# Four attention tiles: transposing on VectorE from 32x32 squares loaded from DRAM

## The chip, the cores and the metric

The kernel runs on one core of one Trainium2 chip. The metric is the device time of one execution in microseconds, as the median of several runs. The profiled execution is a further run, recorded by the hardware profiler; its span goes from the first to the last instruction of the core.

## The reference

Two layers act on 2,048 rows of 1,024 float32 numbers (4 batches of 512):

```
attn = einsum('ds,td->st', w1, w2) * sparse_mask
y    = gelu(einsum('bds,st->bdt', x, attn) + b2)          # exact gelu
x    = layernorm(x + y)
w_l  = dequant_kbit(qweight, lut4, 4)                     # 4 bit planes, 16 values per output row
y    = where(norm(x) > 64, x @ w_h.T, x @ w_l.T) + bias   # w_h: the same with 8 bits
out  = layernorm(x + y)
```

Each row of x is treated on its own, so the order in which a tile holds its rows does not matter as long as the rows come out where they belong.

## The kernel before

**Tiles.** The rows are 16 tiles of 128 (n = 0 to 15), each an SBUF tile `x{n}` with a row per partition, which is loaded once and kept until it is stored. Every tile goes through "attention" (the first layer) and through the second layer. The 1,024 columns are KT = 8 blocks of 128.

**Before the tiles.** In the first 55 us or so the masked product of w1 and w2 is made, only in a band around the diagonal (`attn`), because the mask is zero elsewhere; that it is zero outside the band is checked separately (`check_outside`, L448: a strip of the mask is loaded into a tile called `raw` and its absolute values are summed on ScalarE, L455). The second layer's weights are unpacked from bit planes on ScalarE, VectorE and GpSimd and transposed into `wT`.

**Attention of a tile** (`attention`, L489). Its x must stand transposed, with the contracted columns on the partitions. `transposed` (L438) makes `xT` by eight TensorE transposes into PSUM (L263) and two copies of 128x512 by ScalarE (L264). Then come 20 products with the band (L467, "band" below), the bias added by VectorE (L493, tile `z`), gelu on ScalarE (L494), the residual sum with its row total on VectorE (L498), and the layer norm's numbers: minus the mean (L351, VectorE), the sum of squares (L354, ScalarE, tile `junk`), one over the root (L356 and L357, GpSimd). The row is normalized by L361 on VectorE, which the code keeps in a list (`later`) and issues at a later place (`now()`).

**Second layer.** Tiles 0 to 3 go by halves of the output columns: `ffn_half` has eight products of 128x512 (L512), then VectorE adds the bias and x (L524). The left halves run among the early attention tiles, the right halves R0 to R3 alternate with the attention of tiles 12 to 15; after each right half VectorE makes a sum of weight blocks (L573, 128x2048) which the later tiles need. Tiles 4 to 15 go two at a time (`ffn_pair`, L619) with seven products of half size instead of eight (28 matmuls of L629 a pair, into PSUM tiles u, v and w). Their transposed inputs are made by `squares` (L575): VectorE transposes 32x32 squares within each group of 32 partitions (L579), the result goes to DRAM and comes back with the squares at the partitions where they belong (L583, L589), and ScalarE, VectorE and GpSimd copy, add and subtract them (L611 to L616).

**What sets the order.** A scheduler places the instructions of each engine from the order of the code and its own estimates; from the attention of tile 8 on, VectorE alone keeps the order of the code. Each engine runs its own instructions in order. The loop at L711 goes through `todo`; in each turn it first prepares the transposed input of the next entry. So at the turn of a right half the input of the following attention tile is made.

All loads of x and of the mask strips, the trips of the squares and the stores go through SP's queue in the order in which they stand there; each of these transfers has 128 or 32 rows as its outermost size. Tiles 12 to 15 of x are loaded at the turn of tile 10 (L721), into space that the unpacking has left. In SP's order the mask strips of 186 and 570 columns stand ahead of these loads and those of 314 and 442 columns behind them. The products of attention and of the right halves share two PSUM buffers (`mm`) in turn: a band needs the buffer of the band before, which L493 frees, and a right half the one before, which L524 frees.

Of the kernel before, what the change touches and what calls it, by code (L numbers as in the profile page):

```python
# [9 lines left out]
FP = mybir.dt.float32  # L10
# [7 lines left out]
P = 128  # L18
D = 1024
SOON = 12  # L20
PAIR = 2
KT = D // P
# [8 lines left out]
SQ = 32  # L31
Q = P // SQ
# [160 lines left out]
def kernel(  # L193
# [13 lines left out]
    nc = tc.nc  # L207
    x = x.flatten_outer_dims()
    out = out.flatten_outer_dims()
    NT = x.shape[0] // P  # L210
# [4 lines left out]
    with ExitStack() as main:  # L215
# [42 lines left out]
        def transpose_blocks(dst, block):  # L258

            for g in range(NH):  # L260
                pt = ps_tr.tile([P, HALF // P, P], FP, tag="tr", name="pt")
                for j in range(HALF // P):
                    nc.tensor.transpose(pt[:, j, :], block(g * (HALF // P) + j), ident)  # L263
                nc.scalar.copy(dst[:, g * (HALF // P) : (g + 1) * (HALF // P), :], pt)  # L264

        def transpose_columns(dst, src):
            transpose_blocks(dst, lambda k: src[:, ts(k, P)])
# [60 lines left out]
        def transpose_pending(left):  # L328

            while len(pending) > left:  # L330
                ot, w_nat = pending.pop(0)
                transpose_columns(wT[:, :, ts(ot, P)], w_nat)
# [9 lines left out]
        def steps(n):  # L342
            for _ in range(n):
                next(low, None)


        def stats(u, total):


            nm = work.tile([P, 1], FP, tag="nm", name="nm", bufs=4)  # L350
            nc.vector.tensor_scalar(nm, total, -1.0 / D, None, ALU.mult)  # L351
            junk = work.tile([P, D], BF, tag="junk", name="junk", bufs=1)
            ss = work.tile([P, 1], FP, tag="ss", name="ss", bufs=4)
            nc.scalar.activation(junk, u, AF.Square, bias=nm, accum_out=ss)  # L354
            r = work.tile([P, 1], FP, tag="r", name="r", bufs=4)
            nc.gpsimd.tensor_scalar(r, ss, 1.0 / D, EPS, ALU.mult, ALU.add)  # L356
            nc.gpsimd.tensor_tensor(r, r, minus_half, ALU.pow)  # L357
            return nm, r, ss

        def normalize(dst, u, nm, r):  # L360
            nc.vector.tensor_scalar(dst, u, nm, r, ALU.add, ALU.mult)  # L361

        x_tiles = []

        def load_x(pool, n):
            t = pool.tile([P, D], FP, tag=f"x{n}", name=f"x{n}")
            nc.sync.dma_start(out=t, in_=x[ts(n, P), :])
            x_tiles.append(t)

        attn = band.tile([P, KT, WIN], FP, name="attn")  # L370


        with tc.tile_pool(name="prod", bufs=1) as prod:
# [36 lines left out]
            for n in range(AHEAD):  # L410
                load_x(xp0, n)
# [3 lines left out]
            for s in range(KT):  # L415
# [4 lines left out]
                for k in range(KT):  # L420
                    nc.tensor.matmul(  # L421
                        out=ps[:, : hi - lo],
# [11 lines left out]
        for n in range(AHEAD, SOON):  # L434
            load_x(late, n)
        nc.sync.dma_start(out=bias_bc, in_=bias.partition_broadcast(P))

        def transposed(n, tag, bufs, by_bit):  # L438
            xT = late.tile([P, KT, P], FP, tag=tag, name="xT", bufs=bufs)
            if by_bit:  # L440
                cols = x_tiles[n].rearrange("t (b s) -> t s b", s=8)
                transpose_blocks(xT, lambda k: cols[:, k, :])
            else:
                transpose_columns(xT, x_tiles[n])
            return xT


        def check_outside(s):  # L448

            lo, hi = window(s)  # L450
            raw = work.tile([P, D], FP, tag="z", name="raw", bufs=2)
            for i, (a, b) in enumerate(((0, lo), (hi, D))):
                if a < b:
                    nc.sync.dma_start(out=raw[:, a:b], in_=sparse_mask[ts(s, P), a:b])
                    nc.scalar.activation(  # L455
                        raw[:, a:b], raw[:, a:b], AF.Abs, accum_out=outside[:, 2 * s + i : 2 * s + i + 1]
                    )
# [24 lines left out]
        def now():  # L482
            while later:
                later.pop(0)()
# [4 lines left out]
        def attention(n, xT, meanwhile=nothing):  # L489
            xt = x_tiles[n]  # L490
            ps = band_rows(xT)
            z = work.tile([P, D], FP, tag="z", name="z", bufs=2)
            nc.vector.tensor_tensor(z, ps, b2_bc, ALU.add)  # L493
            nc.scalar.activation(z, z, AF.Gelu)  # L494
            now()
            meanwhile()
            total = work.tile([P, 1], FP, tag="total", name="total", bufs=4)
            nc.vector.scalar_tensor_tensor(xt, z, 1.0, xt, ALU.mult, ALU.add, accum_out=total)  # L498
            nm, r, ss = stats(xt, total)

            def rest():
                normalize(xt, xt, nm, r)

                nc.gpsimd.tensor_tensor(ssq[:, n : n + 1], r, r, ALU.mult)
                nc.gpsimd.tensor_tensor(ssq[:, n : n + 1], ssq[:, n : n + 1], ss, ALU.mult)

            later.append(rest)
# [26 lines left out]
        def finish_rows(n):  # L534
            y = x_tiles[n]
            total = work.tile([P, 1], FP, tag="total", name="total", bufs=4)
            nc.vector.tensor_tensor(total, sums[:, n, 0:1], sums[:, n, 1:2], ALU.add)
            nm, r, _ = stats(y, total)

            def rest():  # L540
                if n < EARLY:
                    o = last.tile([P, D], FP, tag="o", name="o")
                else:
                    o = work.tile([P, D], FP, tag="z", name="o", bufs=2)
                normalize(o, y, nm, r)
                nc.sync.dma_start(out=out[ts(n, P), :], in_=o)

            later.append(rest)

        def ffn_half(n, xT, h):  # L550
            ps = ps_mm.tile([P, D], FP, tag="mm", name="mm")
            product(ps[:, :HALF], xT, h)
            now()
            combine(n, h, ps[:, :HALF], bias_bc[:, ts(h, HALF)])
            if h == 1:
                finish_rows(n)
# [11 lines left out]
        def weight_sum(pool, i):  # L568

            plus, minus = sums_of[i]  # L570
            weights[i] = pool.tile([P, KH, HALF], FP, tag=f"t{i}", name=f"t{i}")
            minus = weights[minus] if isinstance(minus, int) else minus
            nc.vector.tensor_tensor(weights[i], plus, minus, ALU.subtract)  # L573
# [112 lines left out]
        unpack_after = [("attention", 1), ("left", 0), ("attention", 4), ("left", 1)]  # L686
        unpack_after += [("attention", 5), ("left", 2), ("attention", 6), ("left", 3)]

        kept = {}
        rows, blocks = {}, {}  # L690

        def prepare_pair(n, part):

            if n == NT:
                return
            if part < PAIR:
                rows[n + part] = squares(last, n + part)
            else:
                blocks[n] = pair_inputs(last, n, rows[n], rows[n + 1])

        def prepare(what, n):
            if what == "attention":
                return transposed(n, "xT", 2, False)
            if what == "left":
                kept[n] = transposed(n, f"early{n}", 1, True)
            return kept[n]
# [4 lines left out]
        for i, (what, n) in enumerate(todo):  # L711
            if (what, n) == ("left", 0):
                transpose_pending(0)
            if (what, n) == ("attention", 2 * EARLY):
                ordered.enter_context(tc.manual_schedule(engines={mybir.EngineType.DVE}))
            if (what, n) == ("attention", SOON - 2):
                steps(100)
                transpose_pending(0)
                first_sb.close()
                last = main.enter_context(tc.tile_pool(name="last", bufs=1, side="right"))  # L720
                for m in range(SOON, NT):  # L721
                    load_x(last, m)
            xT = ready
            if i + 1 < len(todo):
                ready = prepare(*todo[i + 1])
            if what == "attention":
                if n >= SOON + 1:
                    attention(n, xT, lambda: prepare_pair(EARLY, n - SOON - 1))
                else:
                    attention(n, xT)  # L730
                if n < 2 * EARLY:
                    now()
                if n > 8 and checks < KT:
                    check_outside(checks)
                    checks += 1
            else:
                ffn_half(n, xT, 0 if what == "left" else 1)
                if what == "left" and n > 1:
                    check_outside(checks)
                    checks += 1  # L740
                if what == "right":
                    weight_sum(last, n + 1)
                    now()
            if (what, n) in unpack_after:
                steps(1)
# [57 lines left out]
```

## Time and profile before

| | |
|---|---|
| median of 3 runs | 366.83 us (366.29 to 367.3) |
| the profiled execution | 366.59 us, its span 364.7 us |
| mean granted TensorE clock | 0.966 |
| busy share: TensorE, its weight loads, VectorE, ScalarE, GpSimd | 90%, 55%, 63%, 46%, 23% |
| 8 transposes of an attention tile (L263) and their 2 copies (L264) | 1.04 and 1.04 to 1.07 us in the timeline |
| VectorE transpose L579, 128x1024 float32 | 12 times, 2.03 us in the median |
| loads of x, 512 KB each | 16 times, 6.5 us from issue to landing in the median |
| stores, 512 KB each | 16 times, 2.6 us |

A row of the timeline or of the busy times gives the start and the length in us, the engine, the line of the kernel, the operation with its output and inputs, and in brackets how long the engine had been idle and what ended that. A row by stage gives the stretch, its length, the busy times of PE, PEld (weight loads), DVE, ACT and POOL with the number of instructions, the granted clock, the DMA engines' busy share and GB/s. A row of the chain of waits gives start, length, engine, what it wrote and the line; the chain is followed back from the last instruction, at each step to what released it, or to the instruction before it on its engine. A row of the queues gives packets, MB and the packets' time as a share of 16 DMA engines over the span. PE is TensorE, DVE VectorE, ACT ScalarE, POOL GpSimd.

### The profile page before, as it was taken

Reading aid. Unit: us, or ns where it says so; the run is one execution under the profiler, and the core shown is the slowest. Engines: PE = TensorE matmul, PEld = TensorE weight load, DVE = VectorE, ACT = ScalarE, POOL = GpSimd, SP = SyncE. Lnnn points to the kernel's source line nnn. Section 1 sums busy time; section 2 is a strip of 40 time slices with the busy share of each in tenths; the row PEclk is TensorE's granted clock in tenths of the full one; section 3 lists DMA queues with packets and bytes.
Section 4 is the critical chain, followed back from the end, with each engine's and each line's share of the span. In section 5 each row is a group of like instructions: output and inputs, shape, how many; then the busy total and the mean of one; then the engine's idle time right before and its main releaser. Section 6 shows DMA issues by size and latency. Waiting matters only on the chain.

```text
span 364.7 us, 3670 instructions
## 1 busy us (share of the span) xinstructions
PE 328.5 (90%) x1202; PEld 202.1 (55%) x1202; DVE 231.1 (63%) x351; ACT 166.3 (46%) x242; POOL 83.5 (23%) x130
## 2 busy tenths in 40 slices
PE   4599977989999997999999888999999999999970
PEld 3488866876566586866665433443444444444430
DVE  2589887887988997367676854564635526634130
ACT  0994983989649975675444411301212112012011
POOL 0600420454054111212312440401203004013000
PEclk9699998999999999699999999999999999999995
DMA  9997407700011000812154315143251451432003
GB/s 224 333 373 238 162 2 290 286 2 0 3 46 43 0 3 6 309 44 100 39 176 158 120 58 173 58 177 112 115 180 50 175 170 58 173 117 115 1 4 121
DMA packets 28347, 43.90 MB, mean 120 GB/s; under 512 B 7584, under 2 KB 20640, under 8 KB 28320
## 3 DMA queue, kind: packets, MB, share of 16 engines
q1 hardware_dynamic: 23056, 43.00, 33.3%
q10 hardware_dynamic: 5264, 0.59, 1.2%
q8 instruction: 11, 0.18, 0.2%
q14 instruction: 16, 0.13, 0.1%
HBM read 28.90 MB, written 14.68 MB: 119 GB/s over the span
## 4 chain that ended last, share of the span: by engine, by line
PE 34%; DVE 27%; ACT 16%; issue 8%; DMA 6%; POOL 5%; SPq 1%; ACTq 1%; POOLq 0%; DVEq 0%
PE u L629 16%; PE w L629 8%; ACT junk L354 7%; DVE x L498 5%; PE v L629 4%; DMA rows<-there 3%; DVE e L310 3%; PE mm L467 3%; ACT e L303 3%; DVE z L493 3%; POOL r L357 2%; POOL r L356 2%; DVE root L312 2%; DVE root L311 2%; ACT z L494 2%
## 5 line engine op out<-in xcount | busy, mean ns | idle before, releaser
L354 ACT ACTIVATE junk<-x,nm 128x1024 bf16<-128x1024 f32 x32 | 36.8, 1148 | 66.2 <-DVE nm L351 63.9
L467 PE MATMUL mm<-attn,xT 128*128 128x198 f32 (+2 forms) x320 | 63.7, 357 | 3.0 <-ACT xT L264 3.0
L467 PEld LDWEIGHTS mm<-attn,xT 128*128 128x128 f32 x320 | 55.6, 200 | 10.4 <-ACT xT L264 3.2
L303 ACT ACTIVATE e<-v,lt,diff 128x1024 f32<-128x1024 uint8 x48 | 56.7, 1238 | 6.1 <-DVE v L278 6.1
L512 PE MATMUL mm<-wT,xT 128*128 128x512 f32 x128 | 56.5, 594 | 0.6 <-DVE x L524 0.6
L629 PE MATMUL u<-t,halves 128*128 128x512 f32 x96 | 43.3, 594 | 1.0 <-DVE x L649 1.0
L356 POOL TENSOR_SCALAR r<-ss 128x1 f32<-128x1 f32 x32 | 11.5, 359 | 123.9 <-ACT junk L354 123.9
L512 PEld LDWEIGHTS mm<-wT,xT 128*128 128x128 f32 x128 | 23.7, 190 | 27.7 <-issue 27.4
L307 POOL TENSOR_SCALAR root<-v,diff,lt 128x1024 f32<-128x1024 uint8 x16 | 24.3, 1524 | 58.6 <-DVE v L278 44.0
L629 PEld LDWEIGHTS u<-t,halves 128*128 128x128 f32 x96 | 18.1, 190 | 24.6 <-issue 22.8
L611 ACT COPY halves<-rows 128x1024 f32<-128x1024 f32 x6 | 6.3, 1042 | 55.6 <-DMA rows<-there 55.6
L579 DVE STREAM_TRANSPOSE squares<-x 128x1024 f32<-128x1024 f32 x12 | 24.3, 2026 | 11.5 <-DMA there<-squares 11.5
L421 PE MATMUL mm<-w2T,w_sb 128*128 128x268 f32 (+1 forms) x128 | 30.0, 391 | 0.0
L615 POOL TENSOR_TENSOR halves<-halves 128x512 f32<-128x512 f32 x6 | 9.5, 1584 | 85.4 <-DVE halves L612 85.4
L263 PE MATMUL pt<-ident,x 128*128 128x128 f32 x160 | 22.4, 284 | 7.0 <-ACT wT L264 6.4
L421 PEld LDWEIGHTS mm<-w2T,w_sb 128*128 128x128 f32 x128 | 24.9, 203 | 3.1
L361 DVE TENSOR_SCALAR x<-x,nm,r 128x1024 f32<-128x1024 f32 x16 | 13.0, 812 | 20.4 <-POOL r L357 15.8
L311 DVE COPY_PREDICATED root<-v,e 128x1024 f32<-128x1024 uint8 x16 | 22.5, 1405 | 5.3 <-ACT e L303 4.0
L264 ACT COPY xT<-pt 128x512 f32<-128x512 f32 x40 | 21.0, 585 | 10.3 <-PE pt L263 7.2
L498 DVE SCALAR_TENSOR_TENSOR x<-z,x 128x1024 f32<-128x1024 f32 x16 | 21.5, 1342 | 5.3 <-ACT z L494 5.3
L263 PEld LDWEIGHTS pt<-ident,x 128*128 128x128 f32 x160 | 19.2, 155 | 10.0 <-ACT wT L264 7.8
L494 ACT ACTIVATE z<-z 128x1024 f32<-128x1024 f32 x16 | 16.9, 1054 | 15.8 <-DVE z L493 15.8
(71 smaller groups left out, 434.3 us busy)
## 6 DMA issues: line engine op xcount, KB each, us to landing
x<-in_L_attn_x_dram SPq DMA_DIRECT2D x16, 512.0 KB, 6.5
out_dram<-o SPq DMA_DIRECT2D x16, 512.0 KB, 2.6
there<-squares SPq DMA_DIRECT2D x12, 512.0 KB, 3.0
rows<-there SPq DMA_DIRECT2D x48, 128.0 KB, 2.9
w_raw<-in_L_attn_w_dram SPq DMA_DIRECT2D x8, 512.0 KB, 5.2
w_sb<-in_L_attn_w_dram SPq DMA_DIRECT2D x3, 1024.0 KB, 7.4
w_sb<-in_L_attn_w_dram SPq DMA_DIRECT2D x2, 512.0 KB, 4.9
raw<-_L_attn_sparse_mask_dram SPq DMA_DIRECT2D x2, 413.0 KB, 3.3
```

What stands on the lines that cost most here:

```text
L263: nc.tensor.transpose(pt[:, j, :], block(g * (HALF // P) + j), ident)
L303: nc.scalar.activation(entry[j], plane(0), AF.Identity, scale=d_k, bias=l_k)
L307: nc.gpsimd.tensor_scalar(entry[j], plane(0), d_k, l_k, ALU.mult, ALU.add)
L311: nc.vector.copy_predicated(root, plane(1), entry[1])
L354: nc.scalar.activation(junk, u, AF.Square, bias=nm, accum_out=ss)
L421: nc.tensor.matmul(out=ps[:, : hi - lo], lhsT=w1_sb[s][:, k, :], rhs=w2T[:, k, lo:hi], start=(k == 0), stop=(k == KT - 1),)
L467: nc.tensor.matmul(out=ps[:, a:b], lhsT=xT[:, s, :], rhs=attn[:, s, a - lo : b - lo], start=h not in fresh, stop=hi == D or (h == 0 and wi ...
L494: nc.scalar.activation(z, z, AF.Gelu)
L498: nc.vector.scalar_tensor_tensor(xt, z, 1.0, xt, ALU.mult, ALU.add, accum_out=total)
L512: nc.tensor.matmul(out=ps, lhsT=xT[:, k, :], rhs=wT[:, k, ts(h, HALF)], start=(k == 0), stop=(k == KT - 1),)
L579: nc.vector.transpose(out=t, in_=x_tiles[n].rearrange("t (c j k) -> t c k j", c=Q, k=KT))
L629: nc.tensor.matmul(out=ps, lhsT=a[:, k, :], rhs=b[:, k, :], start=start and k == 0, stop=stop and k == KH - 1, skip_group_check=True,)
```

## The change

For tiles 12 to 15 (SOON = 12), `transposed` no longer uses TensorE and ScalarE. x is loaded a second time, by four loads per tile, each to 32 partitions: partition group g gets, of every four 32-column blocks, the g-th (32 rows x 32 columns pieces of 128 bytes), for the rows 4 i + a with a = 0 to 3 one after the other in the free dimension. VectorE then transposes all 32x32 squares in one instruction, which yields columns on partitions with the tile's rows in the order (a, i). The ordinary tiles `x12` to `x15` are loaded in the same row order, by a rearranged view of DRAM, and their results stored through the same view. Two tiles of squares share one buffer with the weight sums t3 and t4, which are written later. No computation is left out.

```
+        def rows_of(dram, n):
+            rows = dram[ts(n, P), :]
+            return rows if n < SOON else rows.rearrange("(i a) d -> a i d", a=Q)
+
         def load_x(pool, n):
             t = pool.tile([P, D], FP, tag=f"x{n}", name=f"x{n}")
-            nc.sync.dma_start(out=t, in_=x[ts(n, P), :])
+            nc.sync.dma_start(out=t, in_=rows_of(x, n))
             x_tiles.append(t)
+
+        def load_squares(t, n):
+            cols = x[ts(n, P), :].rearrange("(i a) d -> i (a d)", a=Q)
+            cols = cols.rearrange("i (m g j) -> g i m j", g=Q, j=SQ)
+            for g in range(Q):
+                nc.sync.dma_start(
+                    out=t[ts(g, SQ), :].rearrange("i (m j) -> i m j", j=SQ), in_=cols[g]
+                )
...
             xT = late.tile([P, KT, P], FP, tag=tag, name="xT", bufs=bufs)
+            if n >= SOON:
+                nc.vector.transpose(
+                    out=xT.rearrange("p k (a i) -> p a k i", a=Q),
+                    in_=in_squares[n].rearrange("p (a k j) -> p a k j", a=Q, k=KT),
+                )
+                return xT
...
-                nc.sync.dma_start(out=out[ts(n, P), :], in_=o)
+                nc.sync.dma_start(out=rows_of(out, n), in_=o)
...
-                for m in range(SOON, NT):
-                    load_x(last, m)
+                for m in range(SOON, NT, 2):
+                    t = last.tile([P, 2, D], FP, tag=f"t{3 + (m - SOON) // 2}", name="in_squares")
+                    for j in range(2):
+                        in_squares[m + j] = t[:, j, :]
+                        load_squares(in_squares[m + j], m + j)
+                        load_x(last, m + j)
```

More of the change, by code (lines that the diff above doesn't have):

```diff
@@ L687 @@
         unpack_after += [("attention", 5), ("left", 2), ("attention", 6), ("left", 3)]
-        kept = {}
+        kept, in_squares = {}, {}
         rows, blocks = {}, {}
```

## The prediction

> **What bounds the kernel now.** I read the page's slices first (TensorE busy everywhere, its clock granted in full from slice 18 on), then the busy time by stage around the change. The row for one round of a right half and an attention tile:
>
> ```profile
> 165.00:176.40 11.40, 11.40 (x45) 7.20 (x44) 7.16 (x12) 5.61 (x11) 2.72 (x7) 1.00 0.23 80
> ```
>
> TensorE (first figure after the length) is busy for all 11.40 us, so its transposes look like time. The chain of waits says otherwise:
>
> ```profile
> 161.12 1.24 DVE x L498 x2
> 162.98 0.72 issue
> 164.84 0.81 DVE x L361
> 165.65 0.62 DVE x L524 x2
> 166.75 1.25 ACT junk L354 x2
> 168.08 0.81 POOL r L356
> ...
> 170.28 1.23 DVE z L493
> 171.53 1.07 ACT z L494
> 172.62 1.24 DVE x L498 x2
> ```
>
> From 157 to 202 us the chain runs through VectorE, ScalarE and GpSimd and never through TensorE. It goes round once per tile: the L524 that closes a half starts at 165.56, 177.07, 189.29 and 201.50, rounds of 11.51, 12.22 and 12.21 us, while TensorE's bands start 11.33 to 11.34 us apart (165.09, 176.43, 187.76, 199.10). The ring is the slower one already. VectorE's and ScalarE's timelines for tile 11:
>
> ```profile
> 162.38 0.15 DVE L351 TENSOR_SCALAR nm<-total 128x1 f32<-128x1 f32 x1
> 164.84 0.81 DVE L361 TENSOR_SCALAR x<-x,nm,r 128x1024 f32<-128x1024 f32 x1 [2.30 <-POOL r L357]
> ```
> ```profile
> 159.95 0.18 ACT L455 ACTIVATION_READ_ACCUMULATOR raw<-raw 128x1 f32 x1
> 160.04 1.04 ACT L494 ACTIVATE z<-z 128x1024 f32<-128x1024 f32 x1
> 160.99 1.04 ACT L264 COPY xT<-pt 128x512 f32<-128x512 f32 x2
> 162.65 1.15 ACT L354 ACTIVATE junk<-x,nm 128x1024 bf16<-128x1024 f32 x1 [0.62 <-DVE nm L351]
> ```
>
> Between L351 and L361 VectorE idles 2.30 us for the squares' sum (L354) and the root on GpSimd. And ScalarE, in order, sums a mask strip (L455, "raw") just ahead of this work.
>
> **What goes.** Four times eight transposes: a band's start to the next product's was 3.59 + 0.87 us, so 0.87 each, 3.5 us of TensorE, and eight copies of 0.585 us on ScalarE. TensorE's round falls to 10.47 us; the ring's does not. I count only the head start before the first round: without tile 12's transposes the half ends 0.9 us sooner, and the gelu of tile 11 no longer waits behind the strip: the ring could begin 0.9 us earlier.
>
> **The new VectorE transpose.** Nearest row: L579, the same 32x32 transpose of 128x1024 float32, 2.03 us. In the changed program's order it stands after L351 and ahead of L361, in the idle 2.30 us, so it costs nothing; without that cover it would be 4 x 2.03 = 8.1 us. If its runs of 32 make it half as slow again (3.0), 4 x 0.7 = +2.8; if it is as quick as L498 (1.23), nothing, since L361 still waits for GpSimd.
> But GpSimd's L356, due 1.60 us after L351, now runs beside it. This row warns:
>
> ```profile
> 168.08 0.80 POOL L356 TENSOR_SCALAR r<-ss 128x1 f32<-128x1 f32 x1 [2.39 <-ACT junk L354]
> ```
>
> L356 takes 0.19 us alone (175.49), and 0.80 beside L573, ending with it. If the transpose held it too, L361 would come 0.5 us later, four times: +2.0. The Trainium skill (SBUF — State Buffer, Who interferes with whom) says that a VectorE instruction blocks GpSimd when it reads two tensors in SBUF or runs in a two-port mode, not with one input outside such a mode. L573 reads two; the transpose reads one, and at 2.03 us against L361's 0.81 for the same elements it is in no fast mode. I take 0 and keep 2.0 for the range.
>
> **The loads.** Four x loads become 16 loads of squares and four x loads, all on SP, from 145.38. Issued at some 0.45 us (four took 1.79), they keep SP for 9 us instead of 1.8, and behind them stand the loads of the strip that tile 11 waits for (314 and 442 columns), on SP and on the same rings. Queue shares:
>
> ```profile
> q1 hardware_dynamic: 23056, 43.00, 33.3%
> q10 hardware_dynamic: 5264, 0.59, 1.2%
> ```
>
> q10 carries almost only the codes' 128-byte packets: 0.012 x 16 x 364.7 us / 5264 = 13 ns each. A load of squares has 1,024 such packets, 64 per engine: 0.85 us; 16 of them 13.6. From 8.3 to 9.3 us that queue moved 1,654 packets, 9.7 ns each on 16 engines: 9.9 us in all. I take the middle, 11.7. An x load, by the transfers between 146.5 and 154.5 us (about 400 GB/s at full share, 25 per engine, 164 ns a row of 4 KB), costs 8 rows per engine, 1.3 us, **if it is spread over 16 engines**.
> Here a rule speaks against the change. The Trainium skill (DMA: Bandwidth & Descriptors, Why a DMA increments its semaphore by 16 and not by 1): a transfer runs on the largest number of engines, at most 16, that divides the outermost size of both its patterns. "(i a) d -> a i d" puts a = 4 outermost on the DRAM side: four engines, the lowest, for each of the four x loads, and for the last four stores. Then an x load is 32 rows on each of four engines, 5.2 us, four of them 20.8 against 5.2. Every transfer of the trace has 32 or more outermost, so no run here shows it. By the rows alone the strip lands at 146.9 (first x data before) + 11.7 + 5.2 + 1.2 (its own data) + 0.5 (completion) = 165.5; by the rule at 181.1. No row is near such a pattern; I take the rule.
>
> **What waits for it.** ScalarE's order in the changed program: gelu of tile 11, both parts of this strip, then the squares' sum of tile 11. Queued behind the strip is therefore the ring itself: L354, the root, L361, L524. Strip at 181.1, its sums 1.0 us (159.04 to 160.04 before), so L354 of tile 11 starts at 182.1 instead of 162.65: **+19.4**. The round is all VectorE, ScalarE and GpSimd, so nothing gives this back. The PSUM buffer of the next right half is freed only by L524, so TensorE stops from 168 to about 186, and starts at half clock; its round has the room. The next strip is issued only when this one is summed and takes 3.1 us again, before the next L354 at +4.1: no second stall. Squares land in time (tile 15's by about 174).
>
> **After the stage.** The first pair still hangs on L612, L646 and L649, so it moves with the ring. TensorE's order changes there: three v products, not one, go ahead of the first w product. Followed pair by pair (28 products of 0.858 us), pair 1 gains 1.6 us, pair 2 loses 0.7 + 0.65 waiting for L646 and L649 with no v in front and gains the 0.77 of its last wait, and a 1.05 us wait before u<-t,a appears in pairs 3 and 5 where the trace has 0.89 in pair 4: about -0.1 at the end, within 1.2.
>
> **The end.** The last two stores are issued at 355.11 and 358.52 and take 1.2 us of data each (355.95 to 357.1, then from 359.25). On four engines each takes 5.2: the first until 361.2, the second until 366.4 instead of 361.4: **+5.0**. Spread over 16, 0.
>
> **Sum.** Against the profiled execution (366.59; span 364.7): +19.4 - 0.1 + 5.0 = +24.3, 390.9. The median of the three runs is 366.83, 0.24 above; so 391.
>
> **Rivals.**
> Sixteen engines all the same: the strip lands at 165.5, L354 at 166.5, +3.8, no cost at the end: 370.5 (368.5 to 373 with the packet's 9.7 or 13 ns and the transpose's two costs). For it: nothing in the trace shows a transfer held to few engines. Against: none there had four outermost.
> Not slower: the strip arrives before ScalarE needs it. Place: L455 ahead of tile 11's L354. It decides at a landing of 161.7: on 16 engines, 161.7 - 0.5 - 1.2 - 5.2 - 146.9 = 7.9 us are left for the squares, 7.7 ns a packet where the codes' best was 9.7. Then the head start stays: -0.9 - 0.1, 365.8.
> TensorE is the bound after all: 3.5 us of transposes come off, 363.3. For it: the full busy share. Against: it is absent from the chain, and the ring's rounds are longer.
>
> **How the numbers follow.** Four engines 0.74; sixteen 0.18; no stall 0.04; TensorE bound 0.02; slower in another way 0.02. A measurement tells about 0.3% (1.1 us) from no change. Slower 0.94, same 0.04 (365.8 is 0.28% below), faster 0.02. The likeliest's own range is 385 to 397: packets 9.7 to 13 ns (-1.8 to +1.9), the row's 159 to 177 ns (-1 to +2), transpose up to +2.8, GpSimd up to +2.0, tail 1.2. It holds perhaps 0.68; to reach 0.8 the range goes down over the sixteen: 369 to 397.
>
> **What would show it.** In the new trace: the x loads of tiles 12 to 15 take some 5 us more than before from issue to landing; ScalarE idles before L455's counterpart for a DMA, about 20 us, once; VectorE's transpose takes about 2.0 us with little idle left before L361; L356's counterpart stays at 0.19; TensorE has one gap of 18 us near 168; the last store ends 5 us later against the last L361. The prediction fails if the loads with four outermost land like the others, if the strip's sums stand after L354 when run, or if squares are slow enough to delay the transposes themselves.

## The result and the profile after

The changed kernel takes **405.75 us** (median of 4 runs, 405.4 to 408.05) where the kernel before takes 366.72 (4 runs beside it): 1.1086 times as long, 95% interval 1.1062 to 1.1109, or 39 us. The prediction was 391 with a range of 369 to 397: the sign and the place were right, the size was not. The profiled execution has a span of 404.3 us (364.7 before) and a mean granted clock of 0.919 (0.966).

In the changed kernel the lines have new numbers: L520 was L498, L515 was L493, L516 was L494, L546 was L524, L476 and L477 were the strip's load and its sum (L455), L568 the stores, L595 was L573. L354, L356, L357 and L361 are where they were. New are L382 (loads of squares), L373 (loads of x, L367 before) and L457 (VectorE's new transpose).

The busy times by stage, first for the stretch that the prediction showed and then for the same round where it now stands. The columns are the stretch, its length, the busy times of PE, PEld, DVE, ACT and POOL, the granted clock, the share of the DMA engines and GB/s:

```profile
165.00:176.40 11.40, 2.85 (x17) 2.33 (x15) 0.00 (x0) 0.00 (x0) 0.00 (x0) 0.79 0.61 104
195.00:206.40 11.40, 10.11 (x17) 4.40 (x18) 8.40 (x13) 5.65 (x13) 2.72 (x7) 0.68 0.25 83
```

In the first stretch VectorE, ScalarE and GpSimd do nothing at all, and TensorE runs out of work, while the DMA engines are busier than before (0.61 in place of 0.23). The round is run through 30 us later. ScalarE's timeline says what it waited for:

```profile
158.92 1.04 ACT L516 ACTIVATE z<-z 128x1024 f32<-128x1024 f32 x1
191.54 0.47 ACT L477 ACTIVATE raw<-raw 128x314 f32<-128x314 f32 x1 [31.58 <-DMA raw<-_L_attn_sparse_mask_dram]
...
192.65 1.13 ACT L354 ACTIVATE junk<-x,nm 128x1024 bf16<-128x1024 f32 x1
```

The gelu of tile 11 is done at 159.96. Then comes the strip of the mask, and it lands at 191.5. The squares' sum of tile 11 (L354) stands behind it and starts at 192.65, where it started at 162.65: **+30.0**. In SP's timeline (a row joins neighbours of one line, "x4" are four transfers) the four tiles' loads stand ahead of that strip:

```profile
150.42 9.92 SPq L382 DMA_DIRECT2D in_squares<-in_L_attn_x_dram  x4
160.38 0.60 SPq L373 DMA_DIRECT2D x<-in_L_attn_x_dram  x1
161.03 9.84 SPq L382 DMA_DIRECT2D in_squares<-in_L_attn_x_dram  x4
...
183.05 10.52 SPq L476 DMA_DIRECT2D raw<-_L_attn_sparse_mask_dram  x4
```

SP needs 10.5 to 11.5 us for each of the last three tiles and reaches the strip at 183.05. The semaphore records of the trace say which engines it then waits for. A transfer that is spread over 16 engines shows 16 landings there, one of these x loads four (and one record at its issue); the first part of the strip has twelve landings by 186.13 and its last four from 190.75 to 191.52. TensorE's group of the half products has one wait to show for it, all of it for the one L546 that frees the PSUM buffer:

```profile
L534 PE MATMUL mm<-wT,xT 128*128 128x512 f32 x128 | 59.6, 620 | 29.1 <-DVE x L546 29.1
```

TensorE comes back at half clock, as was forecast: the granted clock is 0.50 from 171.6 to 202.3 us, hence the 0.68 in the second row above.

From there on nothing changes. The four right halves start at 195.55, 207.06, 219.28 and 231.51 (before: 165.56, 177.07, 189.29, 201.50), the same rounds to 0.02 us, and the last L361 of the kernel starts 29.96 later (before, then after):

```profile
357.71 0.81 DVE L361 TENSOR_SCALAR o<-x,nm,r 128x1024 f32<-128x1024 f32 x1 [2.30 <-POOL r L357]
387.67 0.81 DVE L361 TENSOR_SCALAR o<-x,nm,r 128x1024 f32<-128x1024 f32 x1 [2.30 <-POOL r L357]
```

After it the span goes on for 16.6 us in place of 7.0: **+9.6**. The two together are the 39.6 us by which the span has grown.

### The profile page after: what moved, and what is told of

Its sections match the earlier page's. It is cut to its first block, busy times and chain, and to the rows that moved or that the text cites. A ratio compares the mean times of both kernels' runs of the same rounds, so it can differ in the third digit from the quotient of the medians.

```text
span 404.3 us, 3623 instructions
## 1 busy us (share of the span) xinstructions
PE 328.7 (81%) x1170; PEld 199.3 (49%) x1170; DVE 235.8 (58%) x355; ACT 162.2 (40%) x234; POOL 85.9 (21%) x130
## 4 chain that ended last, share of the span: by engine, by line
DVE 25%; PE 23%; ACT 14%; SPq 11%; DMA 9%; issue 8%; POOL 5%; ACTq 2%; POOLq 0%; DVEq 0%
PE u L651 11%; SPq L382 8%; ACT junk L354 6%; PE w L651 5%; DMA rows<-there 5%; DVE x L520 4%; DVE e L310 3%; ACT e L303 3%; PE v L651 3%; POOL r L357 3%; DVE squares L601 2%; POOL r L356 2%; DVE root L312 2%; DMA raw<-_L_attn_sparse_mask_dram 2%; DVE z L515 2%
## 5 line engine op out<-in xcount | busy, mean ns | idle before, releaser
L534 PE MATMUL mm<-wT,xT 128*128 128x512 f32 x128 | 59.6, 620 | 29.1 <-DVE x L546 29.1
L489 PE MATMUL mm<-attn,xT 128*128 128x198 f32 (+2 forms) x320 | 64.3, 359 | 5.3 <-ACT xT L264 3.0
L354 ACT ACTIVATE junk<-x,nm 128x1024 bf16<-128x1024 f32 x32 | 36.7, 1148 | 66.8 <-DVE nm L351 64.4
L489 PEld LDWEIGHTS mm<-attn,xT 128*128 128x128 f32 x320 | 55.9, 201 | 13.4 <-ACT xT L264 3.3
L534 PEld LDWEIGHTS mm<-wT,xT 128*128 128x128 f32 x128 | 24.9, 199 | 58.4 <-issue 29.2
L356 POOL TENSOR_SCALAR r<-ss 128x1 f32<-128x1 f32 x32 | 11.5, 358 | 150.9 <-ACT junk L354 150.9
L361 DVE TENSOR_SCALAR x<-x,nm,r 128x1024 f32<-128x1024 f32 x16 | 13.0, 811 | 45.7 <-POOL r L357 41.1
L601 DVE STREAM_TRANSPOSE squares<-x 128x1024 f32<-128x1024 f32 x12 | 24.3, 2028 | 11.4 <-DMA there<-squares 11.4
L516 ACT ACTIVATE z<-z 128x1024 f32<-128x1024 f32 x16 | 16.9, 1055 | 19.9 <-DVE z L515 19.8
L520 DVE SCALAR_TENSOR_TENSOR x<-z,x 128x1024 f32<-128x1024 f32 x16 | 21.4, 1340 | 5.1 <-ACT z L516 5.1
L263 PE MATMUL pt<-ident,x 128*128 128x128 f32 x128 | 17.9, 284 | 7.0 <-ACT wT L264 6.4
L515 DVE TENSOR_TENSOR z<-mm,b_bc 128x1024 f32<-128x1024 f32 x16 | 19.4, 1215 | 6.7 <-PE mm L489 6.7
L310 DVE COPY_PREDICATED e<-v,e 128x1024 f32<-128x1024 uint8 x16 | 22.5, 1405 | 1.4 <-ACT e L303 1.4
```

The lines of the kernel that those rows point to most:

```text
L310: nc.vector.copy_predicated(entry[2], plane(1), entry[3])
L489: nc.tensor.matmul(out=ps[:, a:b], lhsT=xT[:, s, :], rhs=attn[:, s, a - lo : b - lo], start=h not in fresh, stop=hi == D or (h == 0 and wi ...
L534: nc.tensor.matmul(out=ps, lhsT=xT[:, k, :], rhs=wT[:, k, ts(h, HALF)], start=(k == 0), stop=(k == KT - 1),)
L601: nc.vector.transpose(out=t, in_=x_tiles[n].rearrange("t (c j k) -> t c k j", c=Q, k=KT))
```

## The experiments

Seven kernels tell the parts of the change and their causes apart; seven more place its loads otherwise or shorten the ring, to see whether it could be made to pay. Each was timed in turns with the kernel before (366.2 to 366.4 in these series).

### The last four loads and stores in plain order

```
-            nc.sync.dma_start(out=t, in_=rows_of(x, n))
+            nc.sync.dma_start(out=t, in_=x[ts(n, P), :])
...
-                nc.sync.dma_start(out=rows_of(out, n), in_=o)
+                nc.sync.dma_start(out=out[ts(n, P), :], in_=o)
```

> The changed kernel with its last four x loads and last four stores in plain row order (128 outermost); the sixteen squares loads and the VectorE transposes stay. The rows of x that are added, and the rows of the output of the last four tiles, are therefore not in their places. Theory (the pattern with 4 outermost keeps a transfer on four engines, and that is what holds the queue): squares at 13 ns a packet on 16 engines are 13.3 us, the x rows 5.2, the strip's own data 1.7 with its completion: from 147.5 the strip is there at 167.7, the squares' sum L354 of tile 11 starts at 168.7 in place of 192.65 (162.65 before), and nothing is lost at the end: about +5 against before, 372 us (370 to 374). Rival (the squares' 16,384 small packets hold the queue whatever the rows do): SP stays stuck some 10 us in each tile's squares, L354 stays near 190, and only the end is mended: about 396.

Measured: 376.62 us, ratio 1.0282 (1.0264 to 1.0300). ScalarE's timeline (lines as in the changed kernel):

```profile
171.77 0.47 ACT L477 ACTIVATE raw<-raw 128x314 f32<-128x314 f32 x1 [11.96 <-DMA raw<-_L_attn_sparse_mask_dram]
...
172.87 1.13 ACT L354 ACTIVATE junk<-x,nm 128x1024 bf16<-128x1024 f32 x1
```

L354 is 10.2 late, and the end costs nothing (7.0 us after the last L361). So 29 of the 39 us hang on the pattern of eight transfers. The sixteen loads of squares alone cost 10.2, twice the expected 5. Both their terms were too small: 16 x 64 packets of 128 bytes took 16.1 ns each, 16.5 us in place of 13.3, and the rows of x among them 224 ns each, 7.2 us in place of 5.2. From the first square at 147.9 that makes 171.6; the last row ended at 170.6.

### Only the stores in plain order

```
-                nc.sync.dma_start(out=rows_of(out, n), in_=o)
+                nc.sync.dma_start(out=out[ts(n, P), :], in_=o)
```

> The changed kernel with only its last four stores in plain row order (the rows of the last four tiles are then written out of their places); loads as changed. Theory (four engines per store cost 9.6 us after the last L361): the span ends 7.0 us after the last L361 as before, 405.75 - 9.6 = 396.1 (395 to 397.5), with L354 of tile 11 still at about 192.6. Rival (the end is late for another reason, such as SP waiting for earlier transfers): no change, 405.5.

Measured: 394.90 us, ratio 1.0773 (1.0749 to 1.0797), 10.9 less than the changed kernel (10.0 between the profiled spans). L354 of tile 11 still starts at 192.2, and the span ends 7.0 us after the last L361 (387.28 and 394.3). The end term is the stores' alone.

### Only the order of rows, no squares

```
         def load_x(pool, n):
-            nc.sync.dma_start(out=t, in_=x[ts(n, P), :])
+            nc.sync.dma_start(out=t, in_=rows_of(x, n))     # "(i a) d -> a i d", a = 4
...
-                nc.sync.dma_start(out=out[ts(n, P), :], in_=o)
+                nc.sync.dma_start(out=rows_of(out, n), in_=o)
```

> The kernel before with nothing changed but the pattern of its last four x loads and last four stores, which get 4 outermost; no squares are loaded, TensorE transposes all tiles. Theory: the four x loads take 128 rows of 161 to 206 ns on four engines, 20.6 to 26.4 us in a row, so that the strip lands at 146.9 + 20.6 (26.4) + 1.7 = 169.2 (175.0), its sums take 1.0, and L354 of tile 11 starts at 170.2 (176.0): +7.6 (+13.3); with +9.6 at the end 383.8 (389.5). If rows on four engines are slowed only by squares between them, the lower values, and +5.0 at the end: 379.2. Rival (the squares are the cause, four outermost costs nothing): 366.7.

Measured: 388.80 us, ratio 1.0613 (1.0594 to 1.0632). ScalarE's timeline (L461 is the strip's sum here):

```profile
171.07 0.47 ACT L461 ACTIVATE raw<-raw 128x314 f32<-128x314 f32 x1 [12.68 <-DMA raw<-_L_attn_sparse_mask_dram]
...
174.79 1.15 ACT L354 ACTIVATE junk<-x,nm 128x1024 bf16<-128x1024 f32 x1 [0.61 <-DVE nm L351]
```

TensorE transposes everything as before, no square is loaded, and the kernel is 22.6 us slower: L354 of tile 11 starts 12.1 later, the end takes 9.7 more. In the trace's packet records 4.1 rows of 4 KB are under way at every moment from 148 to 169 us (up to 16 in the kernel before), at 175 ns in the mean: 147.6 + 128 x 0.175 = 170.0, and the last row ends at 170.2. A row lay between the two values expected. The strip came at the lower one (169.2 expected), 1.9 later; but in this kernel's order the gelu of tile 11 and two copies stand between the strip and L354, so that 3.7 us pass there and not 1.0. The four loads show four landings each, and the strip behind them twelve by 158.7 and the last four at 169.8 to 171.1. The pattern alone (22.6) and the squares alone (10.4 by the medians) make 33 of the 39 us; the other 6 appear only when both are there.

### 32 outermost, and 8

```
-            return rows if n < SOON else rows.rearrange("(i a) d -> a i d", a=Q)
+            return rows if n < SOON else rows.rearrange("(i a) d -> a i d", a=32)
```

and the same with a=8. The rows are out of their order in DRAM in both.

> As e3_order_only (the kernel before, rows of the last four x loads and stores in another order, TensorE transposes), but with a = 32 in place of 4: the rows are just as much out of their order in DRAM (neighbours on the chip are 32 rows apart), and the pattern has 32 outermost. Theory (the outermost size sets the engines, the order of the rows costs nothing): 16 engines, as before, 366.5 (365.5 to 367.5). Rival (the scattered rows are what was slow in e3_order_only): near its 388.8.

Measured: 366.61 us, ratio 1.0008 (0.9994 to 1.0023). Each x load shows 16 landings. Scattered rows cost nothing; the outermost size does.

> As e3_order_only with a = 8: 8 outermost. Theory: eight engines. The 512 rows of x then take 512 / 8 x 160 to 176 ns = 10.2 to 11.3 us from 147.9, the strip follows at 160 to 161 where ScalarE needs it at 159: L354 of tile 11 +1 to +2; at the end two stores of 16 rows per engine, +0.8 at 160 ns a row and +2.3 at the 235 ns that rows of the stores took on four engines in e3_order_only. Together 368 to 370.5. Rival (four outermost is a special case, eight is spread like 32): 366.5.

Measured: 377.21 us, ratio 1.0297 (1.0272 to 1.0322), so neither: eight engines (eight landings a load, some 8 rows under way at a time), but each row took 265 ns in the mean. L354 of tile 11 came 7.6 late and the end cost 3.5. Eight engines moved 8 x 4,096 bytes in 265 ns, 124 GB/s, four of them 4 x 4,096 in 175 ns, 94. Twice the engines brought a third more. The 235 ns that the expectation takes for rows of stores on four engines are 207 by the packet records; here, on eight, they were 237.

### The x loads on another queue

```
-            nc.sync.dma_start(out=t, in_=rows_of(x, n))
+            (nc.sync if n < SOON else nc.scalar).dma_start(out=t, in_=rows_of(x, n))
```

> The changed kernel with its last four x loads issued by ScalarE, on ScalarE's queue, in place of SP's; patterns as changed. Theory A (the rows on four engines cost so much because squares and strip stand behind them in one queue): without them SP's queue is that of e1_rows_plain, the strip lands at 172 to 179 in place of 191.5, L354 of tile 11 is late by 10 to 17, with the end's 9.6 the time is 386 to 394. Theory B (the four engines themselves are the limit, whichever queue feeds them, since each transfer of squares and strip has a part on them): L354 still late by 25 to 30, 401 to 406.

Measured: 400.90 us, ratio 1.0930 (1.0907 to 1.0952). ScalarE's timeline, then SP's:

```profile
186.44 0.47 ACT L477 ACTIVATE raw<-raw 128x314 f32<-128x314 f32 x1 [20.73 <-DMA raw<-_L_attn_sparse_mask_dram]
...
187.53 1.13 ACT L354 ACTIVATE junk<-x,nm 128x1024 bf16<-128x1024 f32 x1
```
```profile
146.81 36.28 SPq L382 DMA_DIRECT2D in_squares<-in_L_attn_x_dram  x16
```

L354 is 24.9 late, just under theory B's range. SP's queue holds no row of x any more, and SP still needs 36 us for sixteen loads of squares. But this does not settle the two theories, because the queues were not independent: in the built program eight semaphores go round among the transfers of both, and a transfer waits for the earlier one whose semaphore it takes over. SP goes on at 160.93, 166.83, 172.89 and 178.14, and ScalarE's row loads for tiles 12 to 15 landed at 160.92, 166.82, 172.87 and 178.12. That the four engines delay what is wide, even from another queue, shows all the same: the squares issued at 151.59 have twelve landings by 155.97 and their last four at 167.7 to 169.2. The sum over one of these engines fits: from 148.4, 14.2 us of squares and 128 rows of 172 ns (22.0) end at 184.6, and the strip is there at 186.4. A row took 172 ns here, where squares and rows in one queue have 223.

### The exchange of engines without any transfer

```
-                        in_squares[m + j] = t[:, j, :]
-                        load_squares(in_squares[m + j], m + j)
                         load_x(last, m + j)
+                        in_squares[m + j] = x_tiles[m + j]
```

and loads and stores in plain order.

> The changed kernel without any of its loads of squares and in plain row order: VectorE's four transposes read the x tiles themselves, 32x32 square by square, so that the products of the last four tiles get wrong operands; TensorE's transposes of these tiles are gone as in the change. It shows what the exchange of engines is worth when no transfer is touched. Theory (the ring of VectorE, ScalarE and GpSimd is the bound, a transpose of 1.25 us fits in VectorE's idle 2.30): only the head start, 366.7 - 0.9 - 0.1 = 365.7 (365 to 366.5). Rival (TensorE is the bound): 363.2. Rival (VectorE's transposes lengthen the ring): 366.7 + 4 x up to 1.25 = up to 371.7.

Measured: 366.06 us (14 runs), ratio 0.9999 (0.9983 to 1.0016). The busy times of the stretch and VectorE's timeline:

```profile
165.00:176.40 11.40, 10.89 (x38) 6.45 (x37) 8.30 (x13) 4.54 (x9) 2.72 (x6) 1.00 0.23 80
```
```profile
173.90 0.15 DVE L351 TENSOR_SCALAR nm<-total 128x1 f32<-128x1 f32 x1
173.97 1.23 DVE L457 STREAM_TRANSPOSE xT<-x 128x1024 f32<-128x1024 f32 x1
176.36 0.81 DVE L361 TENSOR_SCALAR x<-x,nm,r 128x1024 f32<-128x1024 f32 x1 [1.15 <-POOL r L357]
```

TensorE works 10.89 of 11.40 us where it worked all of them, VectorE does a transpose more, and the right halves start at 165.57, 177.09, 189.31 and 201.53: within 0.03 of before. What the change is about is worth nothing, either way.

### The loads in four portions

```
-                for m in range(SOON, NT, 2):
-                    ...
+                load_last(SOON)                 # one tile's squares and x
+            if what == "right" and n + 1 < EARLY:
+                load_last(SOON + n + 1)
```

> The changed kernel with the same loads issued in four portions: tile 12's squares and x where all stood, tile 13's after the first right half, tile 14's after the second, tile 15's after the third; all patterns as changed. Theory (nothing waits for the squares or x themselves, only for the strip queued behind four tiles' worth of them): behind one tile's worth the strip lands at 147.5 + 3.3 + 6.6 + 1 = 158.5, when ScalarE wants it, and the ring stays where it was; left is the end, +9.6, and up to 3 where a later strip waits behind a portion: 375.7 (375 to 379). Rival (the squares or x of a tile are themselves late, or four engines can't carry them in a round of 12 us): 385 and more.

Measured: 379.72 us, ratio 1.0362 (1.0344 to 1.0380). The stall is gone: L361 of tile 11 starts at 164.51 (164.84 before), the last right half at 201.18 (201.50). No tile's squares or rows are late, on four engines too. The end costs its 9.7. The other 3.6 come at tile 15, and in TensorE's timeline they are not a matter of transfers (a matmul of this kind leaves two records: x8 is one product of half size, and x20 a band, which is thus ten matmuls and not the 20 of the description above):

```profile
200.50 3.70 PE L651 MATMUL u<-wT,halves 128*128 128x512 f32 x8 [2.44 <-ACT halves L633]
204.03 3.60 PE L651 MATMUL v<-wT,halves 128*128 128x512 f32 x8
207.47 3.76 PE L489 MATMUL mm<-attn,xT 128*128 128x198 f32 x20
```

In this kernel the scheduler put two of the first pair's products ahead of tile 15's band (L489), so that its bias (L515) starts at 211.26 in place of 206.22.

### Portions, with each row transfer in four of 32

As above, and

```
-                nc.sync.dma_start(out=rows_of(out, n), in_=o)
+                for a in range(Q):
+                    queue = nc.scalar if a % 2 else nc.sync
+                    queue.dma_start(out=rows_of(out, n)[a], in_=o[ts(a, SQ), :])
```

for the last four stores, and the loads of x alike, on SP.

> As e6_spread, and each of the last four x loads and stores issued as four transfers of 32 rows (32 outermost), the stores on SP's and ScalarE's queue by turns. Theory: with the transfers on 16 engines and no strip behind them, what is left of the change is the exchange of TensorE's transposes for VectorE's, worth nothing by e4_no_squares_loads: 366.2 (365.2 to 367.5), the last store some 0.6 later for its four issues. Rival (TensorE's 3.5 us come to count once nothing stalls): 363. Rival (the squares' small packets, 10.2 us by e1_rows_plain, still cost when spread): 369 to 376.

Measured: 373.00 us, ratio 1.0179 (1.0161 to 1.0196). The end is mended (7.1 us after the last L361). The bias of tile 15 (L519 in this kernel) again waits 5.27 us for TensorE, with the same products ahead of its band. The next kernel issues tile 15's loads together with tile 14's:

```
-            if what == "right" and n + 1 < EARLY:
-                load_last(SOON + n + 1)
+            if what == "right" and n == 0:
+                load_last(SOON + 1)
+            if what == "right" and n == 1:
+                load_last(SOON + 2)
+                load_last(SOON + 3)
```

> As e7_spread_split, but tile 15's loads are issued together with tile 14's after the second right half. In e7_spread_split they stood on SP behind the loads of rows and a strip, and the band of tile 15 (L515's counterpart idle for 5.27 us for TensorE) came 4.3 us late. Theory: that was all that was left of the loads' cost; the rounds to 200 us stood 0.3 ahead of before. 366.2 - 0.3 = 365.9 (365 to 367). Rival (a lasting cost of the squares' packets or of the four-part transfers): 368 to 373.

Measured: 371.91 us, ratio 1.0147 (1.0125 to 1.0169). The expectation named late loads as the reason for the kernel above, and that was wrong: the loads were not late, TensorE's order was. Here that order is right again, and VectorE waits in the same place for something else (L643 is here the first sum for the first pair, L612 in the kernel before, and L524 the residual sum):

```profile
211.74 0.69 DVE L643 TENSOR_TENSOR halves<-rows 128x512 f32<-128x512 f32 x1 [5.00 <-DMA rows<-there]
...
212.96 2.29 DVE L524 SCALAR_TENSOR_TENSOR x<-z,x 128x1024 f32<-128x1024 f32 x1
```

SP issues these loads of rows at 206.07, right behind tile 3's store at 205.64; in the kernel before they are issued at 200.09, ahead of it. To mend that, tiles 0 to 3 were then stored from ScalarE's queue, and the last four tiles' stores issued by SP but for half of tile 15's:

```
-                nc.sync.dma_start(out=rows_of(out, n), in_=o)
+                queue = nc.scalar if n < EARLY else nc.sync       # tiles 0 to 11
...
-                    queue = nc.scalar if a % 2 else nc.sync
+                    queue = nc.scalar if a % 2 and n == NT - 1 else nc.sync
```

> As e9_placed, with two mends of what its trace shows: the loads of rows for the first pair stood on SP behind tile 3's store, so that VectorE's L643 began at 211.74 after 5.00 idle (207.36 before); and the stores issued by ScalarE put 1.1 us ahead of the last tile's squares' sum. The stores of tiles 0 to 3 go to ScalarE's queue, the last four tiles' stores to SP's, those of tile 15 by turns. Theory (the squares' loads cost nothing once nothing waits behind them, and the exchange of engines is worth 0 to 0.3): 366.4 (365.4 to 367.4). Rival (the squares have a lasting cost): 369 to 371.

Measured: 370.80 us, ratio 1.0115 (1.0100 to 1.0129), and again another wait, in SP's timeline:

```profile
172.61 11.77 SPq L377 DMA_DIRECT2D x<-in_L_attn_x_dram  x4
```

These are four loads of tile 14's x. The last of them takes over the semaphore of ScalarE's store of tile 1, which has to wait for VectorE until 181.4; the store has landed at 184.06, and SP issues the load at 184.07. Whether the squares have a cost of their own when no other order is disturbed is therefore not shown as a whole, only up to the last right half: counted from the same L361 (155.09 in the kernel before), the three kernels in portions that precede this one reach it 0.1 to 0.3 us sooner than before.

### A shorter ring, on both sides

VectorE's order in the ring was changed in two ways: the weight sum in two halves, one after a right half's L351 and one while the gelu runs, and the pair's 2.03 us transposes of x after an attention tile's L351.

```
-            nc.vector.tensor_tensor(weights[i], plus, minus, ALU.subtract)
+            k = ts(part, KH // 2)
+            nc.vector.tensor_tensor(weights[i][:, k], plus[:, k], minus[:, k], ALU.subtract)
...
-                    attention(n, xT, lambda: prepare_pair(EARLY, n - SOON - 1))
+                    attention(n, xT, lambda: weight_sum(last, n - SOON + 1, 1))
+                    if n > SOON:
+                        prepare_pair(EARLY, n - SOON - 1)
```

On the kernel before:

> The kernel before with the same changes of VectorE's order (halved weight sums, the pair's transposes after L351), TensorE's transposes kept. Theory (the ring goes below TensorE's round, which then bounds): rounds of 11.34, TensorE's own, in place of 11.51, 12.22 and 12.21: 1.9 in three rounds, 364.3 (363.3 to 365.5). The difference to e10_tuned is then what taking the transposes from TensorE is worth once the ring is shorter, about 1. Rival (the reorder alone is worth as much with TensorE's transposes): 363, no difference.

Measured: **363.01 us** (5 runs, 362.61 to 363.14), ratio 0.9902 (0.9886 to 0.9918): faster than the kernel before and the changed one, by 3.4 and 42.7 us. VectorE's timeline at the right halves (L524 as before the change):

```profile
165.21 0.68 DVE L524 SCALAR_TENSOR_TENSOR x<-mm,bias_bc 128x512 f32<-128x512 f32 x1
176.27 0.69 DVE L524 SCALAR_TENSOR_TENSOR x<-mm,bias_bc 128x512 f32<-128x512 f32 x1
187.61 0.69 DVE L524 SCALAR_TENSOR_TENSOR x<-mm,bias_bc 128x512 f32<-128x512 f32 x1 [0.34 <-PE mm L512]
198.95 0.69 DVE L524 SCALAR_TENSOR_TENSOR x<-mm,bias_bc 128x512 f32<-128x512 f32 x1 [0.34 <-PE mm L512]
```

The rounds are 11.06, 11.34 and 11.34 in place of 11.51, 12.22 and 12.21, and the last two end on TensorE. Of the 3.6 us between the profiled spans 1.0 comes only after the last right half. In this kernel TensorE's transposes could count. The same order on the change with its loads placed, where two of the new transposes move as well:

```
                     weight_sum(last, n + 1, 0)
+                    if 0 < n < EARLY - 1:
+                        kept_xT[SOON + n + 1] = transposed(SOON + n + 1, "xT", 2, False)
```

> As e9_placed, with VectorE's order in the ring changed: the weight sums (two inputs, 2.28 us, beside which GpSimd's L356 takes 0.80 in place of 0.19) are made in two halves, one after a right half's L351 and one while the gelu runs; the pair's transposes of x (single input, 2.03 us) move from the gelu to the idle after an attention tile's L351; the last two tiles' new transposes are made one half earlier. Theory (the ring is the bound; TensorE, without the transposes, has 10.5 of each round's 11.5 to 12.2): rounds of about 11.0 in place of 11.51, 12.22 and 12.21, 2.9 over three rounds: 363.0 (361.5 to 364.5). Rival (TensorE or something behind the ring takes over): 365 to 366.

Measured: 365.71 us (22 runs, 362.29 to 366.58), ratio 0.9982 (0.9970 to 0.9994). The ring does get shorter, the last right half starts at 197.46, 1.5 ahead of the tuned kernel before, but the first pair's loads of rows come late (VectorE's L645 waits 2.59 us for them), and the last L361 starts at 356.03 against 354.16.

And with the stores' queues changed as further above (tiles 0 to 3 from ScalarE's, the last four tiles' from SP's):

> As e10_tuned with the same two mends. In e10_tuned the last right half began at 197.46 (198.95 in e11_before_tuned), but L645 waited 2.59 us for the loads of rows and the last tiles' ends were 1.7 later. Theory (the shorter ring of the change is worth its 1.5 us in the end too): 361.8 (361 to 363). Rival (the products of the pairs bound what follows, whoever transposes): 363.0, as e11_before_tuned.

Measured: 367.03 us (14 runs, 363.87 to 367.98), ratio 1.0008 (0.9994 to 1.0023). The 1.5 us did not reach the end in either form, and both are slower than the kernel before with the same order. Which of the disturbances took them is open; the profiled execution of the last kernel is its fastest run and does not show what the others lost.

## Why the prediction was wrong in size

**The bound.** Right. The ring of VectorE, ScalarE and GpSimd sets the rounds and TensorE does not: the exchange without transfers left the time where it was (0.9999). The head start of 0.9 was too large: with the loads in portions it is 0.1 to 0.3, and in the exchange alone nothing.

**VectorE's transpose.** The step (2.03 us, hidden in 2.30) held in its result. The operation was quicker than its nearest row: 1.25 us where L579 takes 2.03. VectorE's timeline in the changed kernel shows 1.03 us left before L361:

```profile
203.88 0.15 DVE L351 TENSOR_SCALAR nm<-total 128x1 f32<-128x1 f32 x1
204.05 1.25 DVE L457 STREAM_TRANSPOSE xT<-in_squares 128x1024 f32<-128x1024 f32 x1
206.33 0.81 DVE L361 TENSOR_SCALAR x<-x,nm,r 128x1024 f32<-128x1024 f32 x1 [1.03 <-POOL r L357]
```

GpSimd's L356 takes 0.19 us behind it. Since the transpose ends at 205.30 and L356 starts at 205.47, when the squares' sum is there, the two never met, and no run here shows whether one would hold the other. The 2.0 us kept for it in the range were not needed.

**The loads: the term that failed.** The mechanism stood: the strip behind the loads, L354 behind the strip, four engines for a pattern with 4 outermost. With rows alone 4.1 are under way and each load has four landings, with 8 outermost eight, and with 32 outermost sixteen and the cost is gone, as the cited rule says (Trainium skill, DMA: Bandwidth & Descriptors, Why a DMA increments its semaphore by 16 and not by 1). The sum was built right and filled with too small durations. An engine that carries rows has 1,024 packets of squares and 128 rows to move:

| | predicted | measured |
|---|---|---|
| first packet | 146.9 | 147.9 |
| squares | 11.7 us (11.4 ns) | 14.1 us (13.8 ns) |
| rows of x | 20.8 us (163 ns) | 28.6 us (223 ns) |
| strip and its completion | 1.7 us | 0.9 us |
| strip there | 181.1 | 191.5 |

Measured, 147.9 + 14.1 + 28.6 = 190.6, and the last row ended at 190.65. The rows are three quarters of the miss. Their 163 ns came from loads with hardly anything else in the queue. Among squares in the same queue a row took 223 ns on four engines and 224 on sixteen, without them 175 on four, and with the squares in another queue 172. The prediction took the middle for the squares and the undisturbed row for the rest, and its own range for the likeliest case (385 to 397) let a row grow only to 177. A transfer that is moved among others of a new kind has no row of its own in the old trace, and the range should have been kept open there. One more figure was off without a cost of its own: SP was to be done with issuing in 9 us and took 36.7 (146.29 to 182.94). The strip was still issued 7.6 us before the last row ended, so the four engines held it, not SP's issuing.

**The tail.** Right: -0.1 predicted, 192.12 against 192.15 us from the first right half to the last L361. The three v products do stand ahead of the first w product (v x6 at 236.93); the later pairs were not compared one by one.

**The end: also a size.** +5.0 predicted, +9.6 measured, and removed as a whole by plain stores. The data of the last two stores should have taken 10.4 us on four engines. They took 15.5 (386.24 to 401.70): a row was 207 ns in place of 162, which is 64 x 45 ns = 2.9 of the difference of 5.1, and at the end the four engines did not finish together: in the last three microseconds about two were at work, some 2 more.

**The rivals.** That sixteen engines would carry the loads is refuted by the count of rows under way and of landings. That there is no stall is refuted by the 31.58 us. TensorE as the bound is refuted by the exchange alone. Of the signs named, the gap of 18 us on TensorE was 29.1, the idle time on ScalarE 31.58 in place of 20, the last store 9.6 late in place of 5, and VectorE's transpose 1.25 us in place of 2.0; L356 stayed at 0.19, and the one long wait was where it was looked for.

## What to carry to other kernels

Look first for what stands behind a transfer in its queue, then count the engines it can use from the outermost size of both its patterns: a harmless-looking order of rows with 4 outermost cost 22.6 us here, the same disorder with 32 outermost nothing. When transfers of different sizes come to share a queue, cost them per engine, all of them added, and take no duration that was measured alone. And before work is moved off an engine, ask the chain and not the busy share whether that engine bounds: here a shorter ring had to come first, and the new order alone was worth 3.4 us, while moving the transposes on top of it brought nothing to the end.

## Unexpected

- Rows of 4 KB were slower in a queue with 128-byte packets: 223 to 224 ns against 172 to 180. In another queue, on the same four engines, they were not (one run). What does it is open. On sixteen engines most of it sits where a tile's rows begin: the first 64 of the 128 took 226, 324, 354 and 227 ns for the four tiles, and the first 64 of the one load of four tiles in the kernel before took 283. Four beginnings in place of one would account for it there; on four engines the second halves are slow too (164 to 226).
- Eight engines carried rows at 265 ns each, slower than four (175) and sixteen (178 to 180) did. Only one run shows it, and its cause is open.
- Stores of rows on four engines took 207 ns a row with no squares near (163 spread over sixteen), and that too sits at the beginning: some 320 for the first 64 of 256 rows, some 170 for the rest.
- A transfer that takes over a semaphore can be held by a transfer of another engine: moving four stores to ScalarE's queue made SP spend 11.77 us on four loads, and moving the x loads there made SP wait for each of them.
